# Gate read from its PSUM bank, residuals of two 1x1 convolutions moved to VectorE, and new edges of two large convolutions

## Chip, cores and metric

The kernel runs on one core of one Trainium2 chip. The metric is the time of one launch on the device in microseconds. The engines are named as in the profile: PE (TensorE), DVE (VectorE), ACT (ScalarE), POOL (GpSimd) and SP (SyncE, here only a queue that issues DMAs). DMAs are issued by SP, ACT and POOL, each in its own order.

## What is computed

Four layers follow each other on an input x of 8 images, 384 channels and 32 x 32 pixels, all in float32. The reference, cut to what matters:

```python
# layer 0: Mamba in both directions beside a gated depthwise convolution
xn = rmsnorm(x) * norm_w
global_feat = (mamba(xn) + flip(mamba(flip(xn)))) * scale_mod
local_feat = sigmoid(dwconv3x3(xn, dw_w) + dw_b) * xn
x = x + res_scale * (global_feat + local_feat)
...
# inside mamba, per channel d and state n (16 states), along 1024 pixels
h = exp(delta * A) * h + (delta * u) * B
y = sum_n(h * C) + u * D;  y = (y * silu(z)) @ out_proj
...
# layer 1: convolution block, linear attention, MLP
h = cw2 @ bn2(dwconv3x3(cw1 @ bn1(x))) + cb2
x1 = h + x
q, k, v = split(qkv_w @ x1);  kv = phi(k).T @ v
out = (phi(q) @ kv) / (phi(q) @ phi(k).sum())
x2 = x1 + proj_w @ out + proj_b
x = x2 + gelu(layernorm(x2) @ mlp_w1 + mlp_b1) @ mlp_w2 + mlp_b2
...
# layer 2: seven depthwise convolutions (13x13 and six smaller), each with batch norm, summed
# layer 3: pointwise with residual, then a 13x13 depthwise and a GELU
x_pw = bn(pw_w @ x) + x
out = gelu(bn(dwconv13(x_pw)) + bn(x_pw * dw1_w))
```

## The kernel before

Layers 0 and 1 run image by image, layers 2 and 3 on all images at once. A chunk is 128 of the 384 channels (NC = 3), and a half is 512 of the 1024 pixels.

**Scan stage.** `front(b)` normalises image b, projects it, and computes the gate (`branch`) and the inputs of the scan. `scan(b)` holds 48 rounds of exponentials on ACT (L902), products and scans on DVE (L907, L919), products on POOL (L928) and sums on PE (`acc`). `layer1(b)` is layer 1 of one image. While image b is scanned, `front(b + 1)` and `layer1(b - 1)` are interleaved with it. Layer 1 of the last image runs alone after the last scan.

A product of a chunk is written as column quarters (`quarters`, L571) and summed over the three input chunks (`dense`, L580). Its result lies in a PSUM bank: `psum` gives one of two banks ("mm"), used by most products of `front`, the hidden layer of the MLP, k and v; `long_psum` gives one of three ("mo"). The other three hold `du` and `acc`.

**The gate.** In `branch` (L717) the depthwise 3x3 is a product `lc` in a bank. ACT writes tanh of it to an SBUF tile `lg` (L725). One round of the scan loop later `local` (L727) is called; on DVE L728 forms (lg + 1) * xn in `lg`, L731 adds it, times half the residual scale, to the tile `xr`, which goes to x1.

**Residuals.** In the second 1x1 convolution of layer 1 (`c2`, L1048) and in the attention's projection (`pj`, L1147) the residual enters the bank as a product with the identity matrix ahead of the real products. ACT adds the bias while it copies the bank to `xx` (L1052, L1151).

**End of layer 1.** In the MLP a group of hidden chunks (`hm`) is multiplied with the second weight for all three output chunks (`second`, L1247). After the last group `last` (L1217) adds the residual on DVE and stores x2i chunk by chunk from POOL.

**Convolutions a and b.** `conv` (L282) computes a large depthwise convolution as products with Toeplitz rows: 48 steps n of 8 channels each. Per step it needs a window `tp` of 4 x 128 KB (`load_windows`, L239, 20 slots that a and b share) and an input tile `xt`, whose first 32 partitions are loaded by POOL and whose other three shifted copies DVE makes (`shift`, L326, two copies). The first 20 windows of a are loaded by POOL during layer 1 of the last image (L1307). Each step gives two results: `put2` copies one of a to `yt` and POOL stores four together (L382); `put3` applies GELU on ACT to one of b, and POOL stores it (L433).

**Pointwise stage.** Between both, for 16 pairs of image rows t: SP loads `yp` (768 KB), nine products in t's order, ACT (`tm`, L415) and two additions on DVE (L420) fill `xo`, and POOL stores it to xp (L424). After each t the program names one window of b (L426), from the queues of ACT and SP.

**Order.** Engine queues don't follow the program's order. The program is traced twice. `draft` (L1772) hands the first trace to `Plan`, which lays the instructions out on modelled engines; per engine the next one is that with the smallest rank among those that could start within that engine's slack. The rank of every family of instructions, such as `('Pool', 'tp_a<g2_d')`, is shifted by an entry of `BIAS` in ns: a larger one puts it later. The resulting order becomes edges between instructions in the second trace (L2062). Buffers still turn in program order.

Of the kernel before, what the change touches and what calls it, by code (L numbers as in the profile page):

```python
# [17 lines left out]
P = 128  # L18
# [55 lines left out]
def tile_layers(  # L74
# [164 lines left out]
    def load_windows(g_d, tag, n, queues):  # L239

        if not wins:
            wins["pool"] = ctx.enter_context(tc.tile_pool(name="win", bufs=1, side="right"))
        tp = wins["pool"].tile([P, NCH, TP], FP, tag="tp", name=f"tp_{tag}_{n}", bufs=N_WIN)
        for e in range(NSH):
            at = H * ((n % 2 * 2 + e) % NSH)
            win = bass.AP(
                g_d.tensor, g_d[NCH * n, e, 0, 0].offset,
                [[KT, H], [NSH * TG * KT, NCH], [1, TP]],
            )
            queues[e % len(queues)].dma_start(tp[at : at + H], win)  # L250
        wins[tag, n] = tp
# [14 lines left out]
    with tc.tile_pool(name="cx", bufs=2, reuse_waits="tile") as cxp, tc.tile_pool(  # L266
# [15 lines left out]
        def conv(g_d, src_d, last_d, tag, put, far):  # L282
# [13 lines left out]
            def load(n):  # L296
# [10 lines left out]
                if last_d is not None:  # L307
# [12 lines left out]
                src = bass.AP(  # L320
                    src_d.tensor, src_d[NCH * n, 0, 0].offset, [[RL, H], [H * RL, NCH], [1, RL]],
                )
                nc.gpsimd.dma_start(xt[at[0] : at[0] + H], src)
                xts[n] = xt

            def shift(n):  # L326
                at, xt = places(n), xts[n]
                if last_d is not None:
# [45 lines left out]
        def put2(g, ps):  # L374
# [6 lines left out]
            if g % GB == GB - 1:  # L381
                nc.gpsimd.dma_start(y2v[g - GB + 1 : g + 1].rearrange("g p n -> p g n"), hold["t"])  # L382
# [20 lines left out]
        for t in range(H // 2):  # L403
            yt = cwp.tile([P, NC, NB], FP, tag="yp", name=f"yp_{t}", bufs=3)
            nc.sync.dma_start(yt, yf[:, :, t * NB : (t + 1) * NB])
            xo = xos[t % 3]
            for m in range(NC):
                ps = cps.tile([P, HALF], FP, tag="cv", name=f"pw_{t}_{m}")
                for k in range(NC):
                    nc.tensor.matmul(  # L410
                        ps[:, 0:NB], pwt[:, k, m * P : (m + 1) * P], yt[:, k, :],
                        start=(k == 0), stop=(k == NC - 1),
                    )
                tm = cwp.tile([P, NB], FP, tag="tm", name=f"tm_{t}_{m}", bufs=3)
                nc.scalar.activation(  # L415
                    tm, ps[:, 0:NB], AF.Identity, bias=pbias[:, m, :], scale=bns("pw", m)
                )
                for r in range(2):
                    mid = xo[:, m, r, PADW : PADW + B * (W + PADW)].rearrange("p (b w) -> p b w", w=W + PADW)[:, :, 0:W]
                    nc.vector.tensor_add(  # L420
                        mid, tm[:, r * BW : (r + 1) * BW].rearrange("p (b w) -> p b w", w=W),
                        yt[:, m, r * BW : (r + 1) * BW].rearrange("p (b w) -> p b w", w=W),
                    )
            nc.gpsimd.dma_start(xf[:, :, 2 * t : 2 * t + 2, :], xo)  # L424
            if t < N_WIN:
                load_windows(g3_d, "b", t, [nc.scalar, nc.sync])  # L426
# [3 lines left out]
        def put3(g, ps):  # L430
            ot = cxp.tile([P, BW], FP, tag="ot", name=f"ot_{g}", bufs=6)
            nc.scalar.activation(ot, ps, AF.Gelu, bias=gbias[:, g : g + 1])
            nc.gpsimd.dma_start(  # L433
# [8 lines left out]
def _layers01(tc, nc, B, xv, x2_d, x2i_d, dram, ident, mean_w, eps5, eps6, one, half, minus1, vec, bns, bnt,  # L442
# [12 lines left out]
    with ExitStack() as ctx:  # L455
# [124 lines left out]
        def dense(ps, w, m, rhs, begin=True):  # L580
            for k in range(NC):
                product = quarters(
                    ps, w[:, k, m * P : (m + 1) * P], rhs[k] if isinstance(rhs, list) else rhs[:, k, :],
                    begin and k == 0, k == NC - 1,
# [93 lines left out]
        def front(b):  # L678
# [38 lines left out]
            def branch():  # L717
                t3 = tapw(taps3, f"t3_{b}")
                for h in range(2):
                    for c in range(NC):  # L720
# [3 lines left out]
                        lc = t2(f"lg_{b}_{c}_{h}")  # L724
# [9 lines left out]
                        defer(1, local)  # L734
# [267 lines left out]
        def layer1(b):  # L1002
# [43 lines left out]
            for h in range(2):  # L1046
                for m in range(NC):
                    ps = long_psum(f"c2_{b}_{m}_{h}")  # L1048
                    o = xx[h][:, m, :]
                    quarters(ps, ident, o, True, False)  # L1050
                    dense(ps, w, m, dws[h], False)
                    nc.scalar.activation(o, ps, AF.Identity, bias=biasc[:, m, :])  # L1052
# [92 lines left out]
            for h in range(2):  # L1145
                for m in range(NC):
                    ps = long_psum(f"pj_{b}_{h}_{m}")  # L1147
                    o = xx[h][:, m, :]
                    quarters(ps, ident, o, True, False)
                    dense(ps, kvp, m, qps[h], False)  # L1150
                    nc.scalar.activation(o, ps, AF.Identity, bias=vec("proj_b", m))  # L1151
# [46 lines left out]
            behind_gelu = []  # L1198
# [18 lines left out]
            def last(h, acc):  # L1217
                for m in range(NC):
# [4 lines left out]
                    nc.gpsimd.dma_start(x2v[b][:, m, bass.ts(h, HALF)], o)  # L1223
# [4 lines left out]
            for h in range(2):  # L1228
                acc = [long_psum(f"mo_{b}_{h}_{m}") for m in range(NC)]
                for i in range(FF // C):  # L1230
                    wa = wtile(w1_d[:, i * C : (i + 1) * C], f"w1_{b}_{h}_{i}")
                    wb = wtile(w2[i * C : (i + 1) * C, :], f"w2_{b}_{h}_{i}")
                    for fs in [(0, 1), (2,)]:
# [12 lines left out]

                        def second(h=h, i=i, fs=fs, acc=acc, wb=wb, hms=hms):  # L1247
# [12 lines left out]
            behind_gelu.pop()()  # L1260
# [511 lines left out]
def draft(nc, tc, bias):  # L1772
# [15 lines left out]
BIAS = {('Activation', 'acc<y0'): -12600,  # L1788
 ('Activation', 'bc_d<xd'): -51300,
 ('Activation', 'center<center'): -83700,  # L1790
 ('Activation', 'da<dlt'): -200,
 ('Activation', 'dl<dt'): -12400,
 ('Activation', 'dw<dw'): -147300,
 ('Activation', 'fold<fold'): -200,
 ('Activation', 'gbias<biasq_d'): -8800,
 ('Activation', 'h_d<hh'): -8500,
 ('Activation', 'hh<h'): -43100,
 ('Activation', 'hm<mf'): -98200,
 ('Activation', 'kp<phi_k'): 21100,
 ('Activation', 'kv<kvs'): 107600,  # L1800
 ('Activation', 'kvp<kvp'): 156300,
 ('Activation', 'lg<lc'): 39500,
 ('Activation', 'ms_r<ms_r'): 1000,
 ('Activation', 'ms_r<ms_s'): -114400,
 ('Activation', 'phi_k<kv_kp'): 98300,
 ('Activation', 'phi_q<q'): -245400,
 ('Activation', 'rz<den'): 1000,
 ('Activation', 'sq<xi'): -34300,
 ('Activation', 'tm<pw'): -16000,
 ('Activation', 'tp_a<g2_d'): -113400,  # L1810
 ('Activation', 'tp_b<g3_d'): 96300,
 ('Activation', 'u_d<uz'): 29000,
 ('Activation', 'uc<c1'): -700,
 ('Activation', 'uz<in'): -7500,
 ('Activation', 'var_r<var_r'): 1500,
 ('Activation', 'var_r<var_s'): -6000,
 ('Activation', 'vs<xx'): -200,
 ('Activation', 'vt<kv_vt'): 2000,
 ('Activation', 'vt<ones'): 5000,
 ('Activation', 'x2_d<turn'): 72600,  # L1820
 ('Activation', 'xd<xd'): -15500,
 ('Activation', 'xx<c2'): 1700,
 ('Activation', 'xx<pj'): -6000,
 ('Activation', 'yf_d<yt'): 5200,
 ('Activation', 'yt<acc'): -96200,
 ('Activation', 'yt<cv_a'): 32000,
 ('Activation', 'z_d<uz'): 28000,
 ('DVE', 'bias1<fold'): -199800,
 ('DVE', 'bias2<bias2'): 108300,
 ('DVE', 'bias2<bn_t'): -1200,  # L1830
 ('DVE', 'bias3<bn_t'): -28500,
 ('DVE', 'biasc<fold'): 59500,
 ('DVE', 'biasf<fold'): -175000,
 ('DVE', 'carry<hs'): 6400,
 ('DVE', 'dlt<pk'): -14500,
 ('DVE', 'du<vr'): -301300,
 ('DVE', 'dwh<pk'): 31000,
 ('DVE', 'g2<kw'): -17200,
 ('DVE', 'g3<k3'): -159500,
 ('DVE', 'hs<da'): 99000,  # L1840
 ('DVE', 'ks<m8'): -28000,
 ('DVE', 'kv<kvs'): 62700,
 ('DVE', 'lg<lg'): -11200,
 ('DVE', 'ln<xx'): -85600,
 ('DVE', 'pbias<pb'): 52300,
 ('DVE', 'pbias<pbias'): 1000,
 ('DVE', 'qp<qp'): -7200,
 ('DVE', 'uc<dl'): -23400,
 ('DVE', 'ud<uc'): -33200,
 ('DVE', 'v2<pk'): 33500,  # L1850
 ('DVE', 'var_r<var_r'): -67300,
# [217 lines left out]
```

## Time and profile before

| What | Time, us |
|---|---|
| median of 3 runs (lowest to highest) | 4565.5 (4554.0 to 4566.6) |
| the profiled execution | 4564.3 |
| its span, first to last instruction | 4562.5 |
| busy: PE / DVE / POOL / ACT | 4009.3 / 3657.0 / 2771.6 / 2647.7 |
| mean granted clock of PE | 0.924 of full |

The span falls into stages that can be told apart by what the instructions write:

| Stage | From, us | To, us |
|---|---|---|
| preparation of weights, front of image 0 | 0 | 140 |
| scans, with front and layer 1 of the neighbours | 140 | 3610 |
| layer 1 of image 7, its start | 3610 | 3722 |
| layer 1 of image 7, the rest | 3722 | 3972 |
| convolution a | 3982 | 4208 |
| pointwise | 4218 | 4344 |
| convolution b | 4358 | 4556 |

A row of a group gives the line, the engine, the operation, what is written and read, the number of instructions, their busy time and mean duration, and the idle time of the engine just before them with what ended it. A row of a wait gives who waited for whom, the sum in us, the number of times and the longest. Matmuls appear twice per product in the records, since a float32 product is two passes, and four column quarters run beside each other, so eight records are one product of a chunk.

### The profile page before, as it was taken

How to read it: one execution, taken by the hardware profiler on the slowest of the kernel's cores; microseconds unless marked ns; L12 is line 12 of the kernel's file. 1: busy time of each engine (PE TensorE's matmuls, PEld its weight loads, DVE VectorE, ACT ScalarE, POOL GpSimd, SP SyncE). 2: the span in 40 equal slices, each digit the busy share in tenths (PEclk: the TensorE clock that was granted, in tenths of full speed). 3: DMA queues.
4: the chain of work that ended last, by engine and by line, in shares of the span. 5: the costliest groups of instructions: out<-in, count | busy, mean ns of one | idle time of the engine just before them, and what ended most of it. 6: DMA issues, size and time to landing. Idle time of an engine off the chain costs nothing.

```text
span 4562.5 us, 97044 instructions
## 1 busy us (share of the span) xinstructions
PE 4009.3 (88%) x39222; PEld 1573.9 (34%) x39222; DVE 3657.0 (80%) x3749; ACT 2647.7 (58%) x3777; POOL 2771.6 (61%) x1672
## 2 busy tenths in 40 slices
PE   5577699899999999998999999989899789987988
PEld 1122223233433332343223323432232233276467
DVE  2999989999999889998998899899999600175266
ACT  3555657875797578667866786678567413100212
POOL 2677766676667657765776577657676820143079
PEclk8578799999999999999999999999999889998999
DMA  9568776588668866885688668866844761299798
GB/s 259 174 210 273 242 239 209 188 256 264 228 207 254 251 212 204 262 258 198 215 255 249 202 226 261 237 212 215 256 144 162 186 146 48 84 223 229 224 212 183
DMA packets 651130, 975.75 MB, mean 214 GB/s; under 512 B 158280, under 2 KB 333368, under 8 KB 649144
## 3 DMA queue, kind: packets, MB, share of 16 engines
q1 hardware_dynamic: 502064, 676.48, 50.3%
q0 software_dynamic: 53392, 188.07, 13.4%
q10 hardware_dynamic: 95224, 104.98, 7.7%
q8 instruction: 309, 5.06, 0.5%
q14 instruction: 141, 1.16, 0.1%
HBM read 736.63 MB, written 232.67 MB: 212 GB/s over the span
## 4 chain that ended last, share of the span: by engine, by line
PE 42%; issue 15%; DVE 14%; DMA 11%; ACT 6%; POOL 3%; SPq 1%; ACTq 0%; POOLq 0%; DVEq 0%
DVE hs L919 9%; PE mo L575 6%; PE mf L575 6%; DVE du L907 3%; PE pj L575 3%; PE acc L595 3%; PE cv_a L364 2%; PE in L575 2%; PE kv_vt L575 2%; PE c L575 2%; ACT da L902 2%; PE kv_kp L575 2%; DMA tp_a<-g_d 2%; PE q L575 2%; DMA out<-ot 2%
## 5 line engine op out<-in xcount | busy, mean ns | idle before, releaser
L928 POOL TENSOR_TENSOR hs<-hs,bct 128x1024 f32<-128x1024 f32 x768 | 2171.8, 2828 | 845.0 <-DVE carry L924 490.0
L902 ACT ACTIVATE da<-dlt,neg_a 128x512 f32<-128x512 f32 x1536 | 1022.7, 714 | 492.8 <-DVE hs L919 390.6
L907 DVE TENSOR_TENSOR du<-vr,bct 128x1024 f32<-128x1024 f32 x768 | 981.5, 1278 | 49.9 <-DMA vr<-v_d 23.7
L919 DVE TENSOR_TENSOR_SCAN hs<-da,carry,du 128x512 f32<-128x512 f32 x768 | 943.4, 1267 | 37.6 <-ACT da L902 1.0
L919 DVE TENSOR_TENSOR_SCAN hs<-da,du 128x512 f32<-128x512 f32 x768 | 898.3, 1207 | 47.4 <-ACT da L902 15.7
L600 PE MATMUL acc<-hs,selt 128*32 128x512 f32 x2304 | 530.8, 639 | 89.0 <-POOL hs L928 88.9
L575 PE MATMUL mf<-ln,w 128*32 128x512 f32 x4608 | 554.4, 610 | 26.3 <-ACT uc L757 18.6
L575 PE MATMUL mo<-hm,w 128*32 128x512 f32 x4608 | 538.8, 594 | 0.0
L595 PE MATMUL acc<-hs,selt 128*32 128x512 f32 x768 | 416.5, 633 | 41.2 <-POOL hs L928 36.4
L575 PE MATMUL in<-xn,win 128*32 128x512 f32 x2304 | 290.6, 616 | 24.5 <-DMA win<-in_inproj_t 13.9
L902 ACT ACT_TABLE_LOAD x224 | 287.4, 1283 | 40.6 <-DVE hs L919 13.9
L575 PEld LDWEIGHTS mf<-ln,w 128*32 128x32 f32 x4608 | 153.6, 113 | 378.5 <-issue 318.3
L575 PEld LDWEIGHTS mo<-hm,w 128*32 128x32 f32 x4608 | 151.2, 110 | 336.2 <-issue 327.1
L364 PE MATMUL cv_a<-xt_a,tp_a 128*32 128x256 f32 x3072 | 187.2, 398 | 44.8 <-issue 14.7
L1223 POOL DMA_DIRECT2D x2i_d<-xx x48 | 26.6, 555 | 293.8 <-DVE xx L1220 286.3
L364 PE MATMUL cv_b<-xt_b,tp_b 128*32 128x256 f32 x3072 | 180.7, 392 | 26.5 <-DVE xt_b L337 14.2
L600 PE MATMUL dw<-dw_i,t3b 96*32 96x512 f32 x1056 | 192.2, 680 | 10.9 <-DMA dw_i<-h_d 10.7
L337 DVE COPY xt_b<-xt_b 32x2496 f32<-32x2496 f32 x96 | 151.5, 1578 | 50.1 <-DMA xt_b<-xp_d 47.6
L575 PE MATMUL kv_kp<-wk,xx 128*32 128x384 f32 x1536 | 182.2, 487 | 3.9 <-ACT xx L1052 3.7
L364 PEld LDWEIGHTS cv_a<-xt_a,tp_a 128*32 128x32 f32 x3072 | 159.1, 139 | 72.0 <-issue 64.6
L575 PE MATMUL kv_vt<-wv,xx 128*32 128x384 f32 x1536 | 179.7, 491 | 3.8 <-ACT vt L1074 3.8
L600 PEld LDWEIGHTS acc<-hs,selt 128*32 128x32 f32 x2304 | 115.4, 114 | 177.3 <-POOL hs L928 152.3
(211 smaller groups left out, 5855.3 us busy)
## 6 DMA issues: line engine op xcount, KB each, us to landing
dlt<-dl_d SPq DMA_DIRECT2D x384, 256.0 KB, 4.6
vr<-v_d SPq DMA_DIRECT2D x384, 256.0 KB, 5.0
bct<-bc_d SPq DMA_DIRECT2D x256, 256.0 KB, 5.0
ut<-u_d SPq DMA_DIRECT2D x192, 257.5 KB, 5.3
lc_i<-xn_d SPq DMA_DIRECT2D x192, 228.8 KB, 5.9
dw_i<-h_d SPq DMA_DIRECT2D x192, 228.8 KB, 5.8
w<-w_d SPq DMA_DIRECT2D x64, 576.0 KB, 6.3
w<-in_w SPq DMA_DIRECT2D x64, 576.0 KB, 5.0
```

What stands on the lines that cost most here:

```text
L337: nc.vector.tensor_copy(xt[at[e] : at[e] + e * H, :, 0 : RL - e - (e - 1)], xt[at[0] : at[0] + e * H, :, e : RL - (e - 1)],)
L364: nc.tensor.matmul(ps[H * e : H * (e + 1), 0:BW], tp[:, c, :].rearrange("p (j t) -> p j t", t=KT)[:, :, t], rhs, start=(t == 0), stop=(t = ...
L575: product = nc.tensor.matmul(ps[lo:hi], lhs[:, lo:hi], rhs, start=start, stop=stop, skip_group_check=True)
L595: first = product()
L600: tc.keep_in_program_order(product())
L902: nc.scalar.activation(da[:, bass.ts(j, HALF)], dlt[:, bass.ts(j, HALF)], AF.Exp, scale=neg_a[:, g, r : r + 1],)
L907: nc.vector.tensor_mul(pairs(du), pairs(vt), bct[r][:, 0:1, :].to_broadcast([P, 2, HALF]),)
L919: nc.vector.tensor_tensor_scan(t[:, s][:, way], da[:, s][:, way], du[:, s][:, way], k_c if second else 0.0, ALU.mult, ALU.add,)
L928: made.append(nc.gpsimd.tensor_mul(pairs(t), pairs(t), bct[r][:, 1:2, :].to_broadcast([P, 2, HALF])))
L1223: nc.gpsimd.dma_start(x2v[b][:, m, bass.ts(h, HALF)], o)
```

## The change

Five groups of edits:

- **Gate.** Tanh is written back to the product's own bank, and both DVE steps read it there. `local` is called at once, not one turn later.
- **Residuals.** The identity products of `c2` and `pj` are gone. DVE adds bias and residual while it reads the bank, in place of ACT's copy.
- **End of layer 1, last image.** The second products of the last six hidden chunks are kept back and run output chunk by output chunk, each followed by its `last`; stores come from SP.
- **Convolution edges.** The last four results of a are stored one by one from SP. The first two `yp` are loaded chunk by chunk, and their products go over the input chunks first. The last three t run output chunk by output chunk and store xp so, from POOL and SP. Step 0 of b loads all four shifted copies from SP and ACT, and DVE makes none. Results of b are stored from ACT's queue.
- **Windows of b** that the pointwise stage loads get a dependency: those of t may not be issued before the first product of t - 2 has begun.

Besides, every entry of `BIAS` is replaced, the slacks included.

```diff
-    def load_windows(g_d, tag, n, queues):
+    def load_windows(g_d, tag, n, queues, behind=None):
...
-            queues[e % len(queues)].dma_start(tp[at : at + H], win)
+            made = queues[e % len(queues)].dma_start(tp[at : at + H], win)
+            if behind is not None:
+                info = mybir.DependencyInfo(mybir.DependencyClass.NoSync, mybir.DependencyReason.DATA)
+                tc.add_manual_dep(made.ins, behind.ins.name, info, reason="behind")
...
-                nc.gpsimd.dma_start(xt[at[0] : at[0] + H], src)
+                for e in range(NSH if n == 0 else 1):
...
+                    queue = [nc.sync, nc.scalar][e % 2] if n == 0 else nc.gpsimd
+                    queue.dma_start(xt[at[e] : at[e] + H, :, 0 : RL - e], src)
...
+                if n == 0 and last_d is None:
+                    return
...
-            if g % GB == GB - 1:
+            if g >= NQ - GB:
+                nc.sync.dma_start(y2v[g], hold["t"][:, g % GB, :])
+            elif g % GB == GB - 1:
...
+        def fetch(t):
+            yts[t] = cwp.tile([P, NC, NB], FP, tag="yp", name=f"yp_{t}", bufs=3)
+            if t < 2:
+                for k in range(NC):
+                    nc.sync.dma_start(yts[t][:, k, :], yf[:, k, t * NB : (t + 1) * NB])
+            else:
+                nc.sync.dma_start(yts[t], yf[:, :, t * NB : (t + 1) * NB])
...
+        def rows_b(t):
+            if t < N_WIN:
+                load_windows(g3_d, "b", t, [nc.scalar, nc.sync], begun[max(0, t - 2)])
+
+        for t in range(2):
+            fetch(t)
+        for k in range(NC):
+            for t in range(2):
+                for m in range(NC):
+                    product(t, m, [k])
+        for t in range(NT - 3):
+            if t >= 2:
+                fetch(t)
             for m in range(NC):
...
+                if t >= 2:
+                    product(t, m, range(NC))
+                finish(t, m)
+            nc.gpsimd.dma_start(xf[:, :, 2 * t : 2 * t + 2, :], xos[t % 3])
+            rows_b(t)
+        for t in range(NT - 3, NT):
+            fetch(t)
+        for m in range(NC):
+            for t in range(NT - 3, NT):
+                product(t, m, range(NC))
+                finish(t, m)
+                queue = nc.gpsimd if m == 0 else nc.sync
+                queue.dma_start(xf[:, m, 2 * t : 2 * t + 2, :], xos[t % 3][:, m, :, :])
+        for t in range(NT - 3, NT):
+            rows_b(t)
...
-            nc.gpsimd.dma_start(
+            nc.scalar.dma_start(
                 ov[g * P : (g + 1) * P], ot.rearrange("p (b w) -> p b w", w=W)
...
-                        lc = t2(f"lg_{b}_{c}_{h}")
+                        lc = ps
                         nc.scalar.activation(lc, ps, AF.Tanh, bias=dwh[:, c, :], scale=0.5)
...
-                        defer(1, local)
+                        local()
...
                     ps = long_psum(f"c2_{b}_{m}_{h}")
+                    dense(ps, w, m, dws[h])
                     o = xx[h][:, m, :]
-                    quarters(ps, ident, o, True, False)
-                    dense(ps, w, m, dws[h], False)
-                    nc.scalar.activation(o, ps, AF.Identity, bias=biasc[:, m, :])
+                    nc.vector.scalar_tensor_tensor(o, ps, biasc[:, m, :], o, ALU.add, ALU.add)
...
                     ps = long_psum(f"pj_{b}_{h}_{m}")
+                    dense(ps, kvp, m, qps[h])
                     o = xx[h][:, m, :]
-                    quarters(ps, ident, o, True, False)
-                    dense(ps, kvp, m, qps[h], False)
-                    nc.scalar.activation(o, ps, AF.Identity, bias=vec("proj_b", m))
+                    nc.vector.scalar_tensor_tensor(o, ps, vec("proj_b", m), o, ALU.add, ALU.add)
...
-            def last(h, acc):
-                for m in range(NC):
+            def last(h, acc, ms=range(NC)):
+                for m in ms:
...
-                    nc.gpsimd.dma_start(x2v[b][:, m, bass.ts(h, HALF)], o)
+                    (nc.gpsimd if b < B - 1 else nc.sync).dma_start(x2v[b][:, m, bass.ts(h, HALF)], o)
...
+                        if b == B - 1 and h == 1 and i >= FF // C - 2:
+                            rest += [(i, f, hm, wb) for f, hm in zip(fs, hms)]
+                            yield 7
+                            continue
+
...
+            for m in range(NC):
+                for i, f, hm, wb in rest:
+                    quarters(
+                        acc[m], wb[:, f, m * P : (m + 1) * P], hm, False, i == FF // C - 1 and f == NC - 1,
+                    )
+                if rest:
+                    last(1, acc, [m])
...
- ('Pool', 'tp_a<g2_d'): 1000,
+ ('Pool', 'tp_a<g2_d'): 37300,
...
- ('SP', 'turn<x2i_d'): 94400,
+ ('SP', 'turn<x2i_d'): 311100,
...
- ('slack', 'Activation'): 410,
+ ('slack', 'Activation'): 280,
...
```

`product` issues the products of one t, one output chunk and the given input chunks; `finish` holds the lines for `tm` and `xo` as they were.

## The prediction

> **What bounds the kernel now.** I read the span in 40 slices first, then busy time by stage, then the groups by line, then the waits of the stages that are not full. The row of DVE shows three parts: a full one, an almost empty one, and one at five to seven tenths.
>
> ```profile
> span 4562.5 us, 97044 instructions
> PE   5577699899999999998999999989899789987988
> DVE  2999989999999889998998899899999600175266
> 900.00:3500.00 2600.00, 2420.76 (x23552) 857.87 (x23548) 2405.95 (x2394) 1852.58 (x2601) 1753.17 (x875) 0.96 0.73 227
> 3610.00:3722.00 112.00, 74.16 (x469) 18.78 (x461) 10.02 (x12) 7.06 (x11) 54.40 (x89) 0.76 1.01 225
> 3722.00:3972.00 250.00, 241.46 (x2541) 90.26 (x2533) 13.38 (x23) 67.14 (x110) 2.75 (x5) 0.96 0.16 50
> 3972.00:4208.00 236.00, 191.08 (x3094) 163.02 (x3090) 162.20 (x151) 17.57 (x48) 99.19 (x171) 0.93 0.98 219
> 4208.00:4344.00 136.00, 125.87 (x288) 55.42 (x288) 35.77 (x94) 36.84 (x48) 12.01 (x16) 0.95 0.70 216
> 4358.00:4556.00 198.00, 180.72 (x3072) 150.89 (x3072) 148.81 (x95) 43.74 (x96) 185.54 (x137) 0.97 0.97 209
> ```
>
> Columns of the stretches: length, busy PE, PEld, DVE, ACT, POOL, granted clock, DMA share, GB/s. Until 3610 us (scans with layer 1 of the image before) DVE is busy 92.5% and PE 93%: both are near the limit, DVE in order behind its scans. From 3722 to 3972 (layer 1 of image 7) PE alone is full. The first convolution has a DMA share of 0.98 and PE at 81%; the pointwise stage is PE's; in the second convolution POOL is busy 94%.
>
> The groups and waits that the edits touch:
>
> ```profile
> L728 DVE SCALAR_TENSOR_TENSOR lg<-lg,one,xn x48: 721/1707/2885, 299.3 to 2991.4; 128x512 f32<-128x512 f32 x48
> L731 DVE SCALAR_TENSOR_TENSOR xr<-lg,rsh,xr 128x512 f32<-128x512 f32 x48 | 49.5, 1033 | 26.1 <-DMA xr<-in_x 17.5 <-issue 7.2 <-DMA dlt<-dl_d 0.3
> L1017 DVE SCALAR_TENSOR_TENSOR xx<-op,rsm,xx x48: 722/744/752, 531.6 to 3655.1; 128x512 f32<-128x512 f32 x48
> L575 PE MATMUL c<-xx,ident 128*32 128x512 f32 x384 | 73.2, 592 | 0.0
> L433 POOL DMA_DIRECT2D out<-ot x96 | 138.4, 1446 | 15.3 <-DVE xt_b L337 7.6 <-ACT ot L432 7.5
> ACT ot L432 <- DMA out<-ot: 63.7, 45, 5.0
> 4218.13 22.13 PE L410 MATMUL pw<-yp,pwt 128*128 128x512 f32 x46 [10.27 <-DMA yp<-y_d]
> PE cv_b L364 <- DVE xt_b L337: 14.2, 1, 14.2
> PE op L575 <- DMA g<-g_d: 24.1, 1, 24.1
> ```
>
> What to see: L728 (both operands in SBUF) takes 721 to 2885 ns, while L1017, the same operation with one operand in a bank, never exceeds 752. PE stands 10.3 us before the pointwise stage and 14.2 us before the second convolution.
>
> **Part by part.** The profiled execution took 4564.3 us, 1.8 over its span and 1.2 below the median of the runs, so the sum is made against 4564.3.
>
> Gate. L728 (mean 1772 ns) and L731 (1033) now read the bank and should cost 744 each, as L1017: 48 x (1772 + 1033 - 2 x 744) = -63 us of DVE, all in the scan stage. The first also writes the bank, as du (L907) does without harm. A slot of 512 columns (lg) is no longer used.
>
> [...] The trace puts 744 ns beside 721, the fastest from SBUF, thus 2 us, and SBUF's median of 1707 beside both.
>
> Residuals of c and pj. Twelve identity products per image leave PE. Forty records take 4.29 us, eight make one product, so one is 0.858 us: 84 in the scan stage are -72 us of PE, 12 in image 7 are -10.3. ACT loses 96 x 687 ns. DVE gains 96 x 744 ns: 62.5 us in the scan stage. So DVE's work there changes by 62.5 - 63 = about 0. The new wait of DVE for PE has scans and du queued behind it, and POOL's products and the accumulation wait for those. Price: L1017 and L1220 waited 5.4 us for PE in 72 operations from 900 to 3500, hence 84 x 0.08 = 7 us; the upper end is L728's wait for ACT there, 28.5 us in 30, hence 80 us. I take 7, the nearer form.
>
> PE's relief. DVE's idle time with PE named in that stretch adds up to 52 us, 69 over the stage of 3470. The lower end of the gain is 0 (DVE full anyway), the upper all 72 us. I take a third of 69, 23 us, because DVE at 92.5% has little more to give back. With the 7 us the scan stage moves by **-16**, ends -72 and +80.
>
> Planned order. Every entry of the bias table changes, so the order on all queues is new. No row prices that. Images follow each other after 445 to 453 us; 8 us on each of seven is 56 us either way, and that is its bound. I take 0, save in one place: from 3610 to 3722 PE does 74 us of work in 112, waiting for g while POOL issues 80 tp_a loads (10.5 MB, 45 us at 234 GB/s), though DMA then rests at 0.16. The new table ranks those loads on POOL 36 us later. Ends 0 and -38; I take **-15**.
>
> Image 7's layer: -10.3 as above, at full weight because PE is 97% busy. Its last six groups of products go chunk by chunk, 18 x 0.858 = 15.4 us, so the first chunk is stored 10.3 us before PE ends. PE now stands 10.6 us between the last product (3971.4) and conv a (3982.0). Store, load and shift take about 13 us (rows 2 to 5, 4.7, two of 1.45), so 3 us stay and 2 come from the clock, which is halved until 3986.7: **-10**, ends 0 and -12. Both together **-20**.
>
> First convolution. It moves 49.3 MB in 226 us, 218 GB/s, among it 67 tp_b loads (8.8 MB, 40 us at this rate). The tie puts all of them behind the first pointwise product. PE's floor is 384 rounds of 0.427 us, 164. Ends 0 and -62; I take **-31**, since not all of the 40 lies where PE waits.
>
> Into the pointwise stage: single stores on SP, chunked loads, and twelve products that need only two thirds of the channels (10.3 us) lie over the 10.3 us wait: **-12** with the halved clock of 4218 to 4222, ends 0 and -14. SP's yp loads wait for stores with tp_b loads queued behind; nobody needs those yet. The stage takes over the 8.8 MB: 38.2 MB. At its present share of 0.70 for 216 GB/s, a full share is 309 GB/s and 124 us, no loss; at conv a's 218 GB/s it is 175 us, 39 more. I take **+15**.
>
> Into the second convolution: the last three t go chunk by chunk, so 15.4 us of products cover DVE (0.8), store (4.3) and load (4.2), and chunk 0 needs no shift (two of 1.46 us) because four loads bring it: **-13** of the 14.2, ends 0 and -16. The three extra loads of 313 KB add 4 us of traffic at 240 GB/s under that cover.
>
> Second convolution: POOL's cycle was two out issues of 1.77 us and one load of 1.41 a chunk. Out goes to ACT, where a DMA issue of the same size takes 0.32 us (tp_b): 96 x 0.32 = 31 us on an engine busy 44 of 198. Gelu and out then stand behind tp_b loads that wait for a window, as gelu does now (57.5 us). Next late are DVE's shifts (149 us), PE (164) and traffic (41 MB at 245 GB/s, 167). I take 172 for 198: **-26**, ends 0 and -34.
>
> [...]
>
> Sum: -16 - 15 - 20 - 31 - 12 + 15 - 13 - 26 = -118, hence **4446 us**. Of this, -102 is behind 3610 us.
>
> **Rivals.** (1) The scan stage is PE's: all 72 us come off, 4564 - 102 - 72 = 4390. For it: PE 93%; against: DVE is as full and in order. (2) The convolutions are bound by traffic, which the tie only moves: their -67 shrinks to -10, giving 4564 - 16 - 15 - 20 - 10 = 4503. For it: DMA share 0.98 and 0.97; against: POOL's 94% and peaks of 387 GB/s in the pointwise stage. (3) The change doesn't do what it says, because the new order undoes it in the scan stage: +56 for the images' spread, 4564 - 102 + 56 = 4518. (4) Slower: the gate holds its bank. Tanh's bank came free after 0.69 us; now it stays until the second DVE step, and from tanh's end to that step's end passed about 6 us (first and last gate). Only two banks serve all products of the front, the hidden layer and k, v. At 3 us of PE's and so DVE's time per gate it costs 48 x 3 = 144: 4564 - 102 + 144 = 4606. It decides from 102 / 48 = 2.1 us per gate. Against it: PE has products in the three other banks, and the order can put DVE's steps right behind tanh.
>
> **How the numbers follow.** Forecast 0.43, (1) 0.18, (2) 0.17, (3) 0.10, (4) 0.12. The forecast's own range is 4410 to 4485. The range 4385 to 4530 takes in (1), (2) and (3), and leaves out (4) and the edges of (1) and (3), some 0.2. About 0.3% (14 us) is what a measurement of this kernel can tell from no change: faster takes the forecast, (1), (2) and most of (3), 0.84; same 0.04; slower 0.12, that is (4).
>
> **What would show it.** Right: no identity products; the gate's first step at 744 ns; PE's waits of 10.3, 14.2 and 24.1 us below 5 each; no tp_b load before the last cv_a; POOL below 40% in the second convolution and that stage at 170 to 175 us; the scan stage's end 10 to 30 us earlier. Wrong: DVE waiting for c2 and pj by more than 0.5 us each, PE waiting for DVE's gate steps, the pointwise stage above 160 us, or DMA share 1 in a second convolution that stays at 198.

## The result and the profile after

The changed kernel takes 4502.4 us (median of 4 runs, 4501.9 to 4506.5) against 4559.8 us (4552.1 to 4566.6) of the kernel before beside it: ratio 0.9877, interval 0.9856 to 0.9898. It is faster by 1.2%, inside the range that was given, and by about half of the 118 us that were forecast. The profiled execution took 4502.4 us with a span of 4500.4, so 62.1 us of span are to be accounted for.

The page of the changed kernel, busy tenths in 40 slices:

```profile
span 4500.4 us, 95420 instructions
PE   5677789889989999998999899988899969989988
DVE  3999999999899989998999899989989901086274
DMA packets 748722, 976.59 MB, mean 217 GB/s; under 512 B 256840, under 2 KB 433464, under 8 KB 746744
```

The packets under 512 B were 158280 before. The 98560 new ones are 96 x 1024 and some 256 more: each of the 96 stores of `out` is now counted as 1024 pieces of 128 B. With the same stores on POOL's queue (first experiment below) the count is 158536.

Stretches of the changed kernel (length, busy PE, PEld, DVE, ACT, POOL, granted clock, DMA share, GB/s): scan stage, start of image 7's layer, the rest of it, convolution a, pointwise, convolution b.

```profile
140.00:3597.00 3457.00, 3090.26 (x28716) 1110.94 (x28718) 3223.43 (x3287) 2404.48 (x3329) 2372.68 (x1176) 0.93 0.71 225
3597.00:3706.00 109.00, 71.39 (x454) 21.21 (x454) 4.45 (x6) 7.66 (x12) 47.83 (x85) 0.75 0.95 214
3706.00:3943.00 237.00, 219.64 (x2361) 91.74 (x2352) 24.12 (x36) 57.85 (x96) 4.67 (x12) 0.96 0.20 61
3943.00:4137.00 194.00, 175.95 (x3072) 155.75 (x3072) 158.62 (x143) 17.54 (x47) 102.87 (x160) 0.99 0.93 217
4137.00:4261.00 124.00, 119.11 (x288) 53.45 (x287) 32.64 (x90) 33.63 (x45) 10.91 (x15) 0.99 1.00 284
4278.00:4498.00 220.00, 190.10 (x3072) 148.68 (x3072) 134.52 (x95) 45.04 (x96) 42.03 (x44) 0.93 1.03 194
```

Every stage is shorter but the last two. The stretch of the pointwise stage ends before its last products, which run to 4270 us: from its first product to its last the stage takes 130.9 us, 126.0 before. It has a full DMA share, as it took over the windows. In convolution b POOL is nearly free (42 us), yet the stage grew from 204.2 us, counted to the end of the span, to 222.1, and the rate fell to 194 GB/s. The DMA share adds up the times of the packets; at the 1.03 of this stretch they overlap, so it is no occupancy.

The gate and the residuals, groups by line:

```profile
L776 DVE SCALAR_TENSOR_TENSOR lc<-lc,one,xn 128x512 f32<-128x512 f32 x48 | 36.0, 750 | 9.5 <-ACT lc L773 9.1
L779 DVE SCALAR_TENSOR_TENSOR xr<-lc,rsh,xr 128x512 f32<-128x512 f32 x48 | 35.8, 748 | 6.6 <-DMA xr<-in_x 3.2 <-DMA lc_i<-xn_d 1.3 <-DMA dlt<-dl_d 1.0
L1197 DVE SCALAR_TENSOR_TENSOR xx<-pj,pk,xx 128x512 f32<-128x512 f32 x48 | 35.7, 746 | 32.1 <-PE pj L623 32.0
L1099 DVE SCALAR_TENSOR_TENSOR xx<-c,biasc,xx 128x512 f32<-128x512 f32 x48 | 35.7, 743 | 123.1 <-PE c L623 122.9
```

All four cost 743 to 750 ns, as forecast (744). Of L1099's idle time 93.2 us lie in image 7's layer, where PE is busy 291.6 of 347 us.

Waits of the changed kernel in convolution b (who waited for whom, us, times, longest), and the issues of its stores:

```profile
ACT ot L480 <- issue: 44.1, 18, 7.1
PEld cv_b L371 <- ACT ot L480: 35.2, 20, 5.8
PE cv_b L371 <- ACT ot L480: 25.0, 14, 5.4
```

```profile
L481 ACTq DMA_DIRECT2D out<-ot x96: 378/421/7442, 4282.5 to 4497.1; - x96
```

An issue of a store on ACT takes 421 ns in the median but up to 7442. GELU stands behind it (44.1 us of ACT's idle time, for which the profile shows no other wait), and PE stands behind GELU for its bank (25.0 us).

### The profile page after: what moved, and what is told of

The parts are those of the page before. It is cut to its first block, busy times and chain, and to the rows that moved or that the text cites. A ratio compares the mean times of both kernels' runs of the same rounds, so it can differ in the third digit from the quotient of the medians.

```text
span 4500.4 us, 95420 instructions
## 1 busy us (share of the span) xinstructions
PE 3955.7 (88%) x38454; PEld 1607.3 (36%) x38454; DVE 3645.0 (81%) x3843; ACT 2637.5 (59%) x3716; POOL 2635.2 (59%) x1568
## 2 busy tenths in 40 slices
DMA packets 748722, 976.59 MB, mean 217 GB/s; under 512 B 256840, under 2 KB 433464, under 8 KB 746744
## 5 line engine op out<-in xcount | busy, mean ns | idle before, releaser
L623 PE MATMUL mf<-ln,w 128*32 128x512 f32 x4608 | 572.2, 613 | 50.6 <-ACT uc L805 23.5
L623 PE MATMUL mo<-hm,w 128*32 128x512 f32 x4608 | 556.4, 594 | 0.5 <-ACT hm L643 0.5
L623 PEld LDWEIGHTS mf<-ln,w 128*32 128x32 f32 x4608 | 170.8, 113 | 386.3 <-issue 314.0
L623 PEld LDWEIGHTS mo<-hm,w 128*32 128x32 f32 x4608 | 173.8, 110 | 319.2 <-issue 304.2
L313 POOL DMA_DIRECT2D xt_a<-x_d x48 | 41.7, 868 | 339.3 <-PE var_b L623 139.4
L648 PE MATMUL dw<-dw_i,t3b 96*32 96x512 f32 x1056 | 207.2, 678 | 20.5 <-DMA dw_i<-h_d 20.2
L371 PE MATMUL cv_a<-xt_a,tp_a 128*32 128x256 f32 x3072 | 176.1, 385 | 26.9 <-issue 9.6
L344 DVE COPY xt_b<-xt_b 32x2496 f32<-32x2496 f32 x94 | 136.5, 1452 | 73.5 <-DMA xt_b<-xp_d 70.9
L371 PEld LDWEIGHTS cv_b<-xt_b,tp_b 128*32 128x32 f32 x3072 | 148.7, 141 | 78.2 <-ACT ot L480 35.2
L623 PE MATMUL op<-g,wo 128*32 128x512 f32 x1152 | 146.1, 605 | 23.5 <-DMA g<-g_d 23.5
```

What stands on the lines that cost most here:

```text
L313: nc.gpsimd.dma_start(own[:, 0:near], src_d[n].rearrange("h b c w -> h (b c w)"))
L344: nc.vector.tensor_copy(xt[at[e] : at[e] + e * H, :, 0 : RL - e - (e - 1)], xt[at[0] : at[0] + e * H, :, e : RL - (e - 1)],)
L371: nc.tensor.matmul(ps[H * e : H * (e + 1), 0:BW], tp[:, c, :].rearrange("p (j t) -> p j t", t=KT)[:, :, t], rhs, start=(t == 0), stop=(t = ...
L623: product = nc.tensor.matmul(ps[lo:hi], lhs[:, lo:hi], rhs, start=start, stop=stop, skip_group_check=True)
L648: tc.keep_in_program_order(product())
```

## Experiments on the second convolution

Each figure "conv b" counts from the first product of b to the end of the span. It was 204.2 us before and 222.1 after the change. Each comes from one profile; the old code of b took 203.9 to 204.2 us in three profiles, the changed code 220.8 to 228.1 in four (its own and those of the three later experiments that leave b alone and keep the new table).

**Store from POOL again** (the changed kernel, `out` only).

```diff
-            nc.scalar.dma_start(ov[...], ot...)
+            nc.gpsimd.dma_start(ov[...], ot...)
```

> The changed kernel with the results of convolution b stored from POOL again, all else as changed. Theory 1 (pieces): from ACT's queue each store goes as 1024 pieces of 128 B and fills the DMA engines, so with POOL the packets under 512 B fall from 257 to about 158 thousand, convolution b shrinks from 222 us (first product to end) to 195 to 200 and the whole to about 4478. Theory 2 (ACT's order): the issues on ACT hold back GELU; the same size is expected here, with ACT no longer idle behind its own issues. Rival (late windows): convolution b suffers because its Toeplitz rows come later than before; then it stays at 215 to 222 and the whole at 4500.

Measured: 4496.2 us, ratio 0.9876 (0.9849 to 0.9903); conv b 207.3, shorter by 15 us but not the 195 to 200 of both theories.

**Store from SP.**

```diff
-            nc.scalar.dma_start(ov[...], ot...)
+            nc.sync.dma_start(ov[...], ot...)
```

> The changed kernel with the results of convolution b stored from SP. Theory 1 (pieces): SP's queue writes the same 128 B pieces, so packets under 512 B stay at 257 thousand and convolution b at 212 to 222 us, the whole at 4492 to 4502. Theory 2 (ACT's order): ACT is free of the 96 issues, so convolution b falls to 195 to 200 us and the whole to about 4480. Rival (late windows): 222 us.

Measured: 4493.2 us, 0.9861 (0.9846 to 0.9875); conv b 208.2, with 256840 packets under 512 B as in the changed kernel. So about 14 us of the stage go with the issuing on ACT, and the 128-byte pieces alone don't explain the 222.1; the value lies under the band of theory 1 and over that of theory 2.

**Store in pieces of 1 KB, from ACT.** The 256 values of a partition go to one place, so `out` lies in another order than the reference's.

```diff
-            nc.scalar.dma_start(ov[...], ot.rearrange("p (b w) -> p b w", w=W))
+            flat = bass.AP(out.tensor, out[0, 0, 0, 0].offset + g * P * BW, [[BW, P], [1, BW]])
+            nc.scalar.dma_start(flat, ot)
```

> The changed kernel with the results of convolution b stored from ACT, as changed, but each partition's 1 KB in one piece to consecutive addresses; the output is thereby in another order than the reference's. Theory 1 (pieces): packets under 512 B fall to about 158 thousand, the stores take less of the DMA engines, convolution b falls to 190 to 200 us and the whole to 4472 to 4482. Theory 2 (ACT's order): the 96 issues stay on ACT, convolution b stays at 215 to 222 us. Rival (late windows): 222 us.

Measured: 4478.7 us, 0.9827 (0.9812 to 0.9842); conv b 184.9. Same queue, same number of stores, same bytes: longer pieces are worth 37 us. The edit also changes where in `out` the pieces lie (one store now fills 128 KB in a row), and no run tells the length of the pieces from their places. The longest issue on ACT falls from 7442 to 1186 ns with it, so ACT's blocking came with the short pieces too.

**Loads of xt_b from SP, in the kernel before.** The prediction's premise, that POOL's cycle limits the stage, is tested here without any store moved.

```diff
-                nc.gpsimd.dma_start(xt[at[0] : at[0] + H], src)
+                nc.sync.dma_start(xt[at[0] : at[0] + H], src)
```

> The kernel before with one line changed: the xt_b loads of the second convolution are issued by SP, so that POOL, 94% busy there, issues the stores of out alone. Everything else as before. If POOL's cycle was the limit of that stage, as the prediction had it: the second convolution falls from 204.2 us to 170 to 185 us, POOL is under 75% busy there, and the kernel takes 4525 to 4540 us. If the 16 DMA engines are the limit (41 MB at 205 to 220 GB/s, share 0.96 or more whichever queue): 194 to 204 us, the DMA share stays at 0.96 or more although POOL is no longer full, and the kernel takes 4546 to 4560 us.

Measured: 4559.4 us, 0.9987 (0.9972 to 1.0001); conv b 202.6. Its stretch of convolution b, and two waits in it:

```profile
4353.00:4551.00 198.00, 183.23 (x3060) 154.60 (x3064) 154.06 (x96) 45.03 (x95) 123.29 (x94) 0.95 0.97 211
ACT ot L432 <- PE cv_b L364: 141.5, 91, 15.7
POOL out L433 <- ACT ot L432: 83.7, 62, 14.6
```

POOL falls from 94% to 62% busy and the stage stays as long, at a DMA share of 0.97. Before, GELU on ACT waited 63.7 us for stores to land; now it waits for PE's products, and POOL waits for GELU. So with POOL relieved the stage is at once held by something else at the same length: whether POOL held it before or stood beside that other limit, this run doesn't tell, but its relief alone is worth 1.6 us.

**Both at once: stores on POOL, loads of xt_b on SP,** with the tp_a loads held as in the section on image 7.

```diff
-            nc.scalar.dma_start(ov[...], ot...)
+            nc.gpsimd.dma_start(ov[...], ot...)
...
-                    queue = [nc.sync, nc.scalar][e % 2] if n == 0 else nc.gpsimd
+                    queue = [nc.sync, nc.scalar][e % 2] if n == 0 else nc.sync
```

> The changed kernel with the tp_a loads held behind the first c2 product of the last image, out's stores on POOL's queue as before the change, and the xt_b loads on SP, so that POOL issues nothing but the stores in the second convolution. Theory (the stores' 128-byte pieces cost less of the DMA engines on POOL's queue, 59 us against 89, and ScalarE's own issues are gone; what was left to POOL's cycle was the loads): the second convolution takes 185 to 200 us, the kernel 4455 to 4475 us. Rival (traffic of the pieces sets it on any queue): it stays at 205 to 210 us, the kernel at 4470 to 4485. Rival (SP's loads of xt_b stand behind windows that wait): over 215 us.

Measured: 4459.6 us (4459.1 to 4460.4), 0.9785 (0.9764 to 0.9806); conv b 200.3, just above the expected band. This version beats both kernels.

What one store costs can be read from the queues between 4280 and 4450 us (packets, MB, and the time of the packets as a share of 16 engines). The changed kernel, where q10 is ACT's queue with stores and half of the windows, q0 POOL's with the loads of xt_b, q1 SP's with windows alone:

```profile
DMA packets 98827, 35.17 MB, mean 207 GB/s; under 512 B 68889, under 2 KB 96275, under 8 KB 98806
q10 hardware_dynamic: 80421, 15.08, 56.3%
q0 software_dynamic: 3036, 12.17, 29.9%
q1 hardware_dynamic: 15349, 7.60, 21.1%
```

The kernel with stores on POOL and loads on SP, just above, where q0 holds the stores alone:

```profile
q1 hardware_dynamic: 25167, 19.53, 51.9%
q0 software_dynamic: 4038, 11.04, 27.3%
q10 hardware_dynamic: 13620, 6.56, 18.5%
```

The kernel with pieces of 1 KB on ACT:

```profile
q10 hardware_dynamic: 25811, 17.69, 43.0%
q1 hardware_dynamic: 16202, 9.21, 23.2%
```

A store is 0.131 MB. On POOL 11.04 MB are 84 stores, and 27.3% of 170 us are 46.4 us: 0.55 us each. On ACT in the changed kernel some 66 stores (by the packets under 512 B) are 8.65 MB; the other 6.43 MB are windows, at SP's price (35.9 us for 7.60 MB) 30.4 us, which leaves 65.3 us: 0.99 each. In pieces of 1 KB the same working gives 43.9 us for 83 stores: 0.53. So in these three traces 128-byte pieces on ACT's queue cost 0.46 us more a store than pieces of 1 KB, 44 us of packet time over 96. These are estimates: the price of the windows is taken over from SP's queue. On POOL's queue the same store is counted in packets of 2.7 KB on average and is spared this.

**Stores by turns from POOL and SP, tp_b of the pointwise stage from SP alone** (tp_a held too).

```diff
-            nc.scalar.dma_start(ov[...], ot...)
+            (nc.gpsimd if g % 2 else nc.sync).dma_start(ov[...], ot...)
...
-                load_windows(g3_d, "b", t, [nc.scalar, nc.sync], begun[max(0, t - 2)])
+                load_windows(g3_d, "b", t, [nc.sync], begun[max(0, t - 2)])
```

> The changed kernel with the tp_a loads held behind the first c2 product of the last image, out's stores by turns on POOL and SP, the xt_b loads on POOL as in the change, and the tp_b loads of the pointwise stage all from SP. Theory (half of the stores on each queue leaves none of the two full): the second convolution takes 190 to 202 us; with no load on ScalarE's queue, tm does not wait behind loads and the gap into the second convolution is 5 us or less; the kernel takes 4460 to 4475 us. Rival (the pieces set it on any queue): 205 to 210 us, the kernel at 4475 to 4490.

Measured: 4498.4 us, 0.9878 (0.9853 to 0.9903); conv b 229.0, worse than either queue alone. Both expectations missed. The waits in its convolution b:

```profile
ACT ot L482 <- DMA out<-ot: 126.7, 36, 11.4
POOL out L483 <- ACT ot L482: 76.4, 20, 8.8
```

By the profile ACT waits 126.7 us for tiles whose stores have not landed, and POOL 76.4 us for ACT, while its next load of xt_b stands behind the store it waits to issue. Which of the two queues held the tiles was not tried, so the cause of the loss is not shown. The gap into b was 5.7 us (expected: 5 or less), so taking the windows off ACT's queue did not close it. With windows on both queues it was 0.4 in the run above and 8.3 in the changed kernel; its cause stays open.

## Experiments on the scan stage and image 7

**The old bias table** in the changed kernel.

```diff
-BIAS = {('Activation', 'acc<y0'): -14100, ...
+BIAS = {('Activation', 'acc<y0'): -12600, ...
```

> The changed kernel's code planned with the bias table of the kernel before. If the edits themselves made the gain and the table little, as the prediction had it: within 10 us of 4502. If the table made most of it: above 4535. The scan stage, which became 21 us shorter, would then be back at its length of before.

Measured: 4515.0 us, 0.9906 (0.9891 to 0.9921), between the two expectations; the scan stage ends at 3603.6 us (after the change 3596.6). These 7 us say little: the seven versions with the change's code and table in the scan stage (the changed kernel and those with edits behind it) end it at 3592.8 to 3604.1.

**Residuals back on PE,** in the changed kernel.

```diff
-                    dense(ps, w, m, dws[h])
...
-                    nc.vector.scalar_tensor_tensor(o, ps, biasc[:, m, :], o, ALU.add, ALU.add)
+                    quarters(ps, ident, o, True, False)
+                    dense(ps, w, m, dws[h], False)
+                    nc.scalar.activation(o, ps, AF.Identity, bias=biasc[:, m, :])
```

> The changed kernel with the residuals of c2 and pj as identity products on PE again, ACT adding the bias. The prediction's reason (DVE's work is balanced, PE's relief of 72 us gives back 16 to 23 in the scan stage, 10 in image 7): scan stage 15 to 25 us longer, layer of image 7 longer by 10, the whole at 4530. Rival (the scan stage is PE's): 60 to 80 us longer, 4570. Rival (the 50 us for which DVE now waits for c2 and pj cost as much as PE's relief gives): scan stage unchanged within 7, the whole at 4512.

Measured: 4578.1 us, 1.0033 (1.0021 to 1.0045); scan end 3637.2, 40.6 us later, which is none of the three expectations.

**Gate back in an SBUF tile, a turn later,** in the changed kernel.

```diff
-                        lc = ps
+                        lc = t2(f"lg_{b}_{c}_{h}")
...
-                        local()
+                        defer(1, local)
```

> The changed kernel with tanh in an SBUF tile again and the gate's two DVE steps one round later. Theory (DVE is the limit of the scan stage and the two steps take 63 us longer from SBUF): scan stage 35 to 65 us longer, the whole at 4540 to 4565. Rival (the added time lies in DVE's idle time, or the bank is the dearer place): within 10 us of 4502.

Measured: 4562.2 us, 1.0003 (0.9992 to 1.0014); scan end 3655.8.

These two lose 76 and 60 us, more than the whole change gives. But they run under a table made for both edits, so each edit was also made alone in the kernel before, under its own table.

**The gate alone.**

```diff
-                        lc = t2(f"lg_{b}_{c}_{h}")
+                        lc = ps
...
-                        defer(1, local)
+                        local()
```

> The kernel before with the gate's edit alone (factor read from the bank, not deferred), its own bias table and convolutions. Theory (the two edits are a trade between engines: the gate takes 63 us from VectorE, the residuals put 62.5 us back and take 72 us from TensorE): with VectorE relieved and TensorE as loaded as before, the scan stage ends 10 to 40 us earlier, the kernel takes 4520 to 4550 us, and TensorE is the fuller engine. Rival (the table decides: an edit under a table that was not made for it loses more than it gains): the scan stage ends 10 us or more later, the kernel takes 4570 us or more, with new waits on several engines. Rival of the held bank: TensorE waits for the gate's first step, over 1 us a gate.

Measured: 4535.4 us, 0.9951 (0.9935 to 0.9967).

**The residuals alone.**

```diff
-                    quarters(ps, ident, o, True, False)
-                    dense(ps, w, m, dws[h], False)
-                    nc.scalar.activation(o, ps, AF.Identity, bias=biasc[:, m, :])
+                    dense(ps, w, m, dws[h])
+                    nc.vector.scalar_tensor_tensor(o, ps, biasc[:, m, :], o, ALU.add, ALU.add)
```

> The kernel before with the residuals' edit alone (c and pj on VectorE, no identity products), its own bias table and convolutions. Theory (trade between engines): VectorE, 92.5% busy before, gets 62.5 us more in the scan stage and sets its length: the scan stage ends 20 to 60 us later, the layer of the last image is some 20 us shorter, the kernel takes 4560 to 4600 us. Rival (TensorE is the limit of the scan stage): it ends 20 to 70 us earlier, the kernel takes 4470 to 4525 us. Rival (the table decides): later by more than 60 us, and TensorE and VectorE both less busy.

Measured: 4574.1 us, 1.0032 (1.0016 to 1.0048). The scan stages of the kernel before, of the gate alone, and of the residuals alone:

```profile
140.00:3617.00 3477.00, 3125.61 (x29358) 1075.66 (x29360) 3230.19 (x3204) 2413.65 (x3382) 2368.89 (x1178) 0.93 0.71 224
140.00:3591.00 3451.00, 3122.83 (x29310) 1092.01 (x29310) 3177.28 (x3207) 2441.52 (x3403) 2370.79 (x1177) 0.94 0.71 225
```

```profile
140.00:3656.00 3516.00, 3106.25 (x28686) 1060.14 (x28690) 3309.41 (x3290) 2378.45 (x3309) 2369.41 (x1178) 0.93 0.71 221
L728 DVE SCALAR_TENSOR_TENSOR lg<-lg,one,xn 128x512 f32<-128x512 f32 x48 | 100.1, 2085 | 7.8 <-ACT lg L725 7.2 <-DMA xr<-in_x 0.5
```

With DVE 53 us less busy than before (3230 us in 3477) the stage ends 26 us earlier; with DVE 79 us busier it ends 38.5 later, though PE has 84 products fewer. Under the old table, then, DVE's work sets the pace and PE's does not. Under the new table this doesn't hold alone: with the residuals back on PE, DVE is busy 3179.7 us, 44 less than in the changed kernel, and the stage ends 40.6 us later. Under the gate alone DVE is still the fuller engine (92.1% against 90.5% of PE), not PE as expected.

Where the scan stage ends, us:

| Bias table | neither | gate | residuals | both |
|---|---|---|---|---|
| of before | 3617.5 | 3591.5 | 3656.0 | 3603.6 |
| of after | not run | 3637.2 | 3655.8 | 3596.6 |

In this stage the residual edit costs 38.5 us under the old table without the gate; the 12 us with it are hardly more than the scatter of 11 us named above. It pays in image 7's layer, which takes 350.3 us with it alone, 371.1 with the gate alone, 364.5 before. And a table is worth 46 us to one set of instructions (3591.5 against 3637.2) and nothing to another (3656.0 against 3655.8).

**tp_a held behind the first c2 product of the last image,** and issued by ACT, in the changed kernel.

```diff
-            load_windows(g2_d, "a", n, queues)
+            load_windows(g2_d, "a", n, queues, late_start["c2"])
...
-        ahead = windows([nc.gpsimd])
+        ahead = windows([nc.scalar])
...
-            next(ahead, None)
+            if "c2" in late_start:
+                next(ahead, None)
```

> The changed kernel with the first 20 windows of convolution a (80 loads, 10.5 MB) tied behind the first product of c2 of image 7 and issued from ACT, in place of POOL at that layer's start. Theory (these loads hold back g and the shifted images of the 3x3): the layer of image 7 (end of the scans to first product of convolution a) falls from 347 us to 315 to 325 and PE's wait of 23.5 us for g goes below 10; the whole at 4475. Rival (the start of that layer waits for its own chain of store and load, whatever else is on the DMA engines): 340 to 347 us, the whole at 4500 or later.

Measured: 4487.3 us, 0.9838 (0.9812 to 0.9864); the layer of image 7 takes 321.8 us in place of 346.8. The tie and the other issuer were not tried apart. Waits at its start, changed kernel first, then this one with the stretch that follows the last scan:

```profile
PE op L623 <- DMA g<-g_d: 23.5, 1, 23.5
```

```profile
ACT phi_k L1049 <- DMA tp_a<-g_d: 35.0, 5, 13.0
PE op L625 <- DMA g<-g_d: 10.8, 1, 10.8
3604.00:3711.00 107.00, 89.59 (x844) 34.39 (x848) 7.45 (x10) 13.90 (x27) 1.23 (x6) 0.92 0.90 192
```

In the changed kernel POOL still issued its 80 loads from 3598.4 us on, at once after the last scan: the new table did not put them behind g. Held back, they cost ACT a wait of 35 us for windows, but no wait of PE for ACT is among the seven longest sums there, of which the 10.8 us for g is the least, and PE is busy 84% of the stretch at clock 0.92, in place of 65% at 0.75.

## Why the prediction was right in direction and wrong in size

| Step | Forecast, us | Measured on the two profiles, us |
|---|---|---|
| scan stage | -16 | -20.9 |
| start of image 7's layer and its rest | -15 - 20 | -17.7 |
| convolution a | -31 | -31.8 |
| into pointwise | -12 | -8.6 |
| pointwise and into b | +15 - 13 | +4.9 - 5.9 |
| convolution b | -26 | +17.9 |
| sum | -118 | -62.1 |

**Convolution b is the step that failed:** 44 of the 56 us missing. Two of its statements fell. First, that the stage falls to 172 us once "POOL's cycle" is relieved: relieved alone, it gave 1.6 us, and PE, put at 164 (384 rounds of 0.427 us; in the trace of before eight rounds of b at their closest follow each other in 3.45 us, 0.43 each), was busy 180.7 us of the 198 in the prediction's own row. From its first to its last product of b PE stood idle for only 12.3 us before, and in no run was it busy there for less than 176.3 us. The cycle itself was mis-added too: two issues of 1.77 us and one load of 1.41 make 238 us over 48 chunks, more than the stage, since the issues of out took 1446 ns in the mean. Second, out on ACT was priced at 0.32 us an issue, from loads of the same size. The issues blocked ACT for up to 7.4 us, and the short pieces added some 0.46 us of packet time a store. No run had shown a store of out from ACT's queue when this was forecast: the kernel before stores from POOL's queue, where the pieces are not counted as 128-byte packets at all (3951 packets under 512 B from 4360 to 4556 us, with all 96 stores in it). The time to landing doesn't show the price either: 6.6 us in the median from POOL before and 5.0 from ACT, while the stage grew by 17.9 us. On ACT's queue it took 184.9 us with pieces of 1 KB against 222.1, and with pieces of 128 B the queue mattered (207.3 us on POOL, 208.2 on SP, 222.1 on ACT).

**The start of image 7's layer** gave next to nothing of its -15: of the bounds 0 and -38 the first nearly held (112 us became 109). The rank in the table, 36 us later, did not keep the loads behind g: they were issued from 3598.4 us on, and PE still waited 23.5 us for g (24.1 before). With an edge, and ACT as the issuer, the layer became another 25 us shorter. The rest of the layer then gave about 15 of its 20.

**The scan stage** was near in sum, but by terms that cancel. The gate's operations cost what was said (750 and 748 ns; the 2 us of the prediction are 744 less 721 ns, 96 times). The new wait for c2 and pj was 50 us (29.6 and 20.7), not 7, inside the bound of 80; the gate's own waits fell by 48 at the same time (37.6 and 26.1 before), which was not foreseen. PE's relief of -23 is not seen as such: PE's busy time in the stage fell by 35 us (3125.6 to 3090.3), not by 72, and under the old table it is DVE's work that moves the stage. The new order, taken at 0, gave 7 us against the old table, within the scatter.

**Convolution a** met its number on the pair of profiles, but the same code of a took 225.2, 211.9, 212.5 and 219.5 us in the four profiles without the tie (mean 217.3), and 193.2 to 201.6 in the nine with the tie under the change's own table (mean 196.1). The tie goes with about 21, the rest of the 31.8 is this pair's scatter. The two groups differ in their tables as well; with the tie under the old table 198.9 us passed from the first product of a to the first of the pointwise stage, as in the nine (195.5 to 204.0) and not as in the four (223.3 to 236.1, of which the wait into pointwise makes 8 more), so the table is not what did it.

**Pointwise and the way into b** came out at -1.0 for the forecast +2, by luck: neither term met its number (+4.9 for +15, -5.9 for -13), and the errors cancel. From the first pointwise product to the first of b passed 140.2 us before and 137.9 to 143.1 in every version with the tie under its table. That what the edges gained was taken by the moved windows is likely, but no run has one without the other.

**The rivals.** That the convolutions are bound by traffic came nearest in time (4503), by chance: it took 35 us off image 7's layer, where 17.7 came off, and 10 off the convolutions, where 23.5 came off. For b the price of the pieces (0.46 us a store on ACT's queue, by the estimate above) speaks for it; for a it was wrong in that moving 8.8 MB did help, as the pointwise stage had a DMA share of only 0.70. The rival of a scan bound by PE fell, for the old table, with the residuals alone (slower). For the gate's first step nothing waited, for the second PE 9.3 us in seven waits and POOL, which stores its result, 24.6 us: of the 144 us put on the held bank PE's waits show 9.3 at most. That the new order would undo the gain was not seen either.

What stays open: what limits convolution b at 200 to 208 us when the stores come from POOL. The DMA share is 0.96 to 0.99, and in the best version PE is busy 180.9 of the 194.6 us from its first to its last product; the two were not separated.

## What to carry to other kernels

Before moving a store to another queue, look at the length of its pieces on that queue: the count of packets under 512 B in the profile (here 256840 against 158536) says what a busy row cannot. Relieving a full engine pays only if nothing else stands at the same length (here it gave 1.6 us), and a run of the old kernel with one line moved tells that before anything is rebuilt. Where an order matters, write it as a dependency; a rank moved by a tuned table may change nothing (here the 80 loads still began at 3598.4 us, at once after the last scan), and an edit tried under a table made for another one shows the table too.

## What the runs showed of the hardware

- The same 128 KB store to rows of 128 B is counted as 1024 packets from ACT's or SP's queue and as packets of 2.7 KB on average from POOL's. By the working above that is 0.99 us of packet time a store on ACT's queue and 0.55 on POOL's.
- An issue of a 128 KB store on ACT took 421 ns in the median and up to 7442 with pieces of 128 B; with pieces of 1 KB the longest was 1186.
- Two steps of DVE cost 1772 and 1033 ns before and 750 and 748 with an operand in PSUM; with the residuals added on DVE and the gate left in SBUF the first rose to 2085.
